# Biases carried inside the weights: a one in place of normalized xn's first feature

## The chip, the cores and the metric

The kernel runs on one core of a Trainium2 chip, in float32 for all products. The metric is the device time of one execution in microseconds. A core has these engines: TensorE (PE, matrix products; its weight loads are shown apart as PEld), VectorE (DVE, elementwise work and reductions), ScalarE (ACT, activation functions and copies with scale and bias), GpSimd (POOL, elementwise work) and SyncE (SP, which here only issues DMA transfers). Each takes its own instructions in order. SBUF is the on-chip memory. PSUM holds what TensorE produces[...].

## The reference

The source `x` has 4 batches of 2048 tokens with 256 features. Everything is computed from the row-normalized tokens `xn = layernorm(x)`. Two branches read them and their product is added to `x`:

```
x = src;  xn = layernorm(x)                    # per token, over 256 features, no scale and shift
q = xn @ Wq + bq;  k = xn @ Wk + bk;  v = xn @ Wv + bv     # 16 heads of 64
Q = elu(q) + 1;  K = elu(k) + 1
KV = sum over tokens of K v^T                  # per batch and head, 64 x 64
Z = 1 / (Q . (sum over tokens of K) + 1e-6)
o = Q KV Z;  attn = o @ Wo + bo
x1 = layernorm(xn + attn) * g1 + be1
s = layernorm(x1 + gelu(x1 @ W1 + b1) @ W2 + b2) * g2 + be2
g = silu(fp4_linear(silu(fp4_linear(xn, w_gate)) * fp4_linear(xn, w_up), w_down))
out = x + s * g
```

`fp4_linear` rounds both operands to a 4-bit grid with one scale for every 16 elements. This linear attention needs a whole batch's KV and key sums before any of that batch's queries can be finished.

Two facts of the reference matter. The mean of a row of `xn` over its features is zero, so its first feature is minus the sum of the others. And `elu(z) + 1` equals `max(z + 1, min(exp(z), 1))`.

## The kernel before, in words

**Tiling.** The 8192 tokens are cut into 32 blocks of 256 tokens (two tiles of 128, `TB` = 2), eight blocks per batch. Work on keys is done in two halves `f` of 512 of the 1024 key features. In PSUM, four buffers with the tag "mm" serve in turn nearly all products, and four hold sums over many products (`pxk` of a half, and the FFN's sums).

**Keys.** For a batch, the kernel does not form v. It sums `xn^T K` over all tokens (`pxk`, 256 by 512 per half) and multiplies by Wv afterwards. `key_product` makes pk = xn Wk for one tile and half (two matmuls of 512 columns), DVE adds bk + 1 (row `k<-pk,bk`, line 495) and ACT takes Exp of k − 1 (line 497). `key_elu` takes min with 1 and max with k on DVE (`kk`, line 504), and GpSimd adds kk to `kacc` (lines 506 and 508), an elementwise running sum that is later summed over its 128 partitions. `key_xk` multiplies xn^T by kk onto `pxk`.

**End of a batch's keys.** `m_of_half` (line 540) turns the sums of one half into `m`, which applied to Q gives attention already multiplied by Wo. ACT copies pxk to `xk`; TensorE sums kacc over partitions with a column of ones (`pks`, line 562); ACT copies the row to `krow`; SyncE stores it to `k_d` in DRAM and loads it back spread over all partitions (`ksum`). From ksum DVE builds `own`, `kcol` and the columns of `kh`, which give the denominators by matmul (`pz`). TensorE multiplies xk by Wv (`pkv`), eight small DVE operations add bv times ksum (`kv`, line 600), TensorE multiplies by Wo (`pm`), ACT copies to `m`. It is a generator: `step` moves it to its next `yield`, and so a few products at a time stand between the others.

**Queries.** `q_of` (line 763) makes four PSUM tiles pq for a block, each of two 128-feature columns. ACT copies each with its bias, bq + 1 (Identity, line 782, two per tile), into `q1`, takes Exp (line 785), and DVE takes min and max (`zq`, line 789). `q1` has three buffers, which keys and queries share.

**Stages.** A prologue works the keys of batch 0 in eight steps, with the quantizing of the gate and up weights between (to about 131 us). A transition makes the first `m` and starts block 0 (to about 185 us). Blocks 0 to 23 each carry two half-blocks of the keys of the next batch beside their own attention and FFN (some 57 us each). Blocks 24 to 31 have no keys beside them (some 44.5 us each).

**The xn of the next batch.** `keys_norm` normalizes a block of keys on DVE and stores it to DRAM as `xn_d`, from where the queries and the second half f load it again. `keys_xnT` (prologue) transposes it on TensorE. `keys_apart` and `keys_T` (later) do that by splitting float32 into 16-bit halves (`apart`, on ACT) and by transposing DMA transfers.

**Order.** TensorE takes instructions in program order. For DVE and ACT a scheduler keeps program order through the prologue, and from line 1040 (`in_order[0] = False`) chooses by priority; `tc.issue_after(i)` keeps an instruction behind another. Transfers stand in one SyncE queue. `load_when(dep, ...)` (line 129) holds a transfer back until `dep` is done: a one-element GpSimd copy writes into its destination first. Rows of the profile with L115 are DVE or ACT operations recorded by a helper, L99 matmuls, L102 transposes on TensorE.

Of the kernel before, what the change touches and what calls it, by code (L numbers as in the profile page):

```python
# [22 lines left out]
def linear_attention_gated_by_fp4_ffn(  # L23
# [23 lines left out]
):  # L47

# [93 lines left out]
    bk1 = const.tile([P, HD], F32, name="bk1")  # L142

    def load_wk(f, eng):
        fs = slice(f * HALF, (f + 1) * HALF)
        eng.dma_start(wk_sb[:, :, fs], wk_r[:, :, fs])
        eng.dma_start(bk1[:, fs], as_rows(bk[fs]))

    load_wk(0, nc.scalar)
    load_x(1)  # L150
    load_wk(1, nc.scalar)

# [10 lines left out]
    ones = const.tile([P, P], F32, name="ones")  # L163
# [29 lines left out]
    def w2_sums():  # L193
# [8 lines left out]
        2: [lambda dep: load_when(dep, wq_sb, by_chunks(Wq))],  # L202
        3: [lambda dep: load_when(dep, w1_sb, by_chunks(W1))],
        4: [
            lambda dep: load_row("g1", g1, dep),
# [4 lines left out]
        5: [lambda dep: load_w2(dep)],  # L210
    }

# [8 lines left out]
    def small_constants():  # L221


        vs = (("bq", bq), ("b1", b1), ("bv", bv), ("g1", g1), ("be1", be1))
        n = sum(v.shape[0] // P for _, v in vs)
        brow = work.tile([n, P], F32, tag="z", name="brow", bufs=1)
        r = 0
        for name, v in vs:
            k = v.shape[0] // P
            nc.sync.dma_start(brow[r : r + k, :], v.rearrange("(c p) -> c p", p=P))  # L230
            cols[name] = (r, r + k)
            r += k
        yield
        pb = mm_tile("pb")
        tr(pb[:, :n], brow, ident[:n, :n])
        bcol = const.tile([P, n], F32, name="bcol")
        vector.tensor_copy(bcol, pb[:, :n])
        for name, (lo, hi) in cols.items():
            cols[name] = bcol[:, lo:hi]
        vector.tensor_scalar(cols["bq"], cols["bq"], 1.0, None, ALU.add)  # L240
        yield
# [168 lines left out]

    def keys_norm(n, mv, rstd):

        xn = work.tile([P, TB, D], F32, tag="xn_k", name=f"xn_k_0_{n}", bufs=3)
        normalize(xn, x_k.pop(n), mv, rstd)
        xn_d[n] = dram.tile([P, TB, D], F32, tag="xn_d", name=f"xn_d_{n}")
        nc.sync.dma_start(xn_d[n], xn)
        return xn

    def keys_xnT(n, xn):
        xnT = work.tile([P, ND, T], F32, tag="xnT_k", name=f"xnT_k_0_{n}", bufs=3)  # L420
        scalar.copy(xnT, transposes(xn, f"k_{n}"))
        store_xnT(n, xnT)
        return xnT
# [18 lines left out]
    def keys_apart(b, sub, issue=None):  # L442

        f, bi = divmod(sub, NB)
        if f > 0:
            return
        n = b * NB + bi
        half = keys[b, sub][0].bitcast(U16).rearrange("p j (c f h) -> p h c j f", c=ND, h=2)
        apart = work.tile([P, 2, ND, TB, P], U16, tag="e", name=f"apart_{n}", bufs=3)
        with tc.issue_after(issue) if issue is not None else nullcontext():  # L450
            for h in range(2):
                scalar.copy(apart[:, h], half[:, h])
        apartT = work.tile([P, 2, ND * T], U16, tag="kk", name=f"apartT_{n}", bufs=3)
        nc.sync.dma_start(
            apartT.rearrange("p h (m t) -> p (h m) t", t=P),
            apart.rearrange("p h c j f -> p (h c j f)"),
            transpose=True,
        )
        keys[b, sub].append(apartT)

    def keys_T(b, sub, issue=None):

        f, bi = divmod(sub, NB)
        if f > 0:
            return
        n = b * NB + bi
        xn, *apartT = keys[b, sub]
        xnT = work.tile([P, ND, T], F32, tag="xnT_k", name=f"xnT_k_0_{n}", bufs=3)
        if apartT:
            with tc.issue_after(issue):  # L470
                scalar.copy(
                    xnT.bitcast(U16).rearrange("p c (t h) -> p h (c t)", h=2), apartT[0]
                )
        else:
            scalar.copy(xnT, transposes(xn, f"k_{n}"))
        store_xnT(n, xnT)
        keys[b, sub] = [xn, xnT]

    def key_sums(b, f, tag):
        keys[b, "acc", f] = batch.tile([P, HALF], F32, tag="kacc", name=f"kacc_{b}_{f}")  # L480
        keys[b, "pxk", f] = [acc_tile(f"pxk_{b}_{f}_{d}", tag) for d in range(ND)]

    def key_product(xnT, f, j, nm):

        fs = slice(f * HALF, (f + 1) * HALF)
        pk = mm_tile(f"pk_{nm}_{j}")
        for c in range(ND):
            mm(
                pk, xnT[:, c, j * P : (j + 1) * P], wk_sb[:, c, fs],
                start=c == 0, stop=c == ND - 1,  # L490
            )
        k1 = work.tile([P, HALF], F32, tag="q1", name=f"k1_{nm}_{j}", bufs=3)

        with tc.issue_after(keys["kh"]) if "kh" in keys else nullcontext():
            vector.tensor_tensor(k1, pk, bk1[:, fs], ALU.add)
        e = work.tile([P, HALF], F32, tag="e", name=f"ek_{nm}_{j}", bufs=3)
        keys["exp"] = scalar.activation(e, k1, AF.Exp, bias=neg_one).ins
        return k1, e

    def key_elu(b, f, k1, e, nm, first):  # L500

        kacc = keys[b, "acc", f]
        kk = work.tile([P, HALF], F32, tag="kk", name=f"kk_{nm}", bufs=3)
        ins = vector.scalar_tensor_tensor(kk, e, 1.0, k1, ALU.min, ALU.max)
        if first:
            acc = nc.gpsimd.tensor_copy(kacc, kk)
        else:
            acc = nc.gpsimd.tensor_tensor(kacc, kacc, kk, ALU.add)  # L508
        pool["last"] = acc.ins
        return kk, ins.ins  # L510
# [5 lines left out]
    def keys_k(b, sub):  # L516
# [5 lines left out]
        for j in range(TB):  # L522
            nm = f"{b}_{sub}"
            kk, ins = key_elu(
                b, f, *key_product(xnT, f, j, nm), f"{nm}_{j}", bi == 0 and j == 0
            )
# [13 lines left out]
    def m_of_half(b, f, dep=None, ahead=False):  # L540
# [3 lines left out]
        fs = slice(f * HALF, (f + 1) * HALF)  # L544
        wv = batch.tile([P, ND, HALF], F32, tag="wv", name=f"wv_{nm}", bufs=1)
        load_when(dep, wv, by_chunks(Wv)[:, :, fs])
# [8 lines left out]
        kacc = keys.pop((b, "acc", f))  # L555
        pxk = keys.pop((b, "pxk", f))
        xk = batch.tile([P, ND, HALF], F32, tag="xk", name=f"xk_{nm}", bufs=1)
        for d in range(ND):
            scalar.copy(xk[:, d, :], pxk[d])

        pks = mm_tile(f"pks_{nm}")
        mm(pks[:1, :], ones[:, 0:1], kacc, start=True, stop=True)
        krow = work.tile([P, HALF], F32, tag="x1T", name=f"krow_{nm}", bufs=1)[:1, :]
        scalar.copy(krow, pks[:1, :])
        k_d = dram.tile([1, HALF], F32, tag="k_d", name=f"k_d_{nm}", bufs=2)
        nc.sync.dma_start(k_d, krow)
        yield
        ksum = work.tile([P, 4, P], F32, tag="x1", name=f"ksum_{nm}")
        nc.sync.dma_start(
            ksum, k_d.rearrange("o (c f) -> o c f", c=4).to_broadcast([P, 4, P])  # L570
        )

        own = work.tile([P, 4, P], F32, tag="kk", name=f"own_{nm}", bufs=3)
        kcol = small.tile([P, 4], F32, tag="kcol", name=f"kcol_{nm}")
        vector.tensor_tensor(own, ksum, ident.unsqueeze(1).to_broadcast([P, 4, P]), ALU.mult)
        vector.tensor_reduce(kcol, own, AX.X, ALU.add)
        for i in range(2):
            hs = slice(i * DH, (i + 1) * DH)
            r0 = 2 * f + i
            ins = vector.tensor_copy(kh[b][hs, 4 * f : 4 * f + 4, r0], kcol[hs, :])  # L580
            if f > 0:
                keys["kh"] = ins.ins
# [13 lines left out]
        for ci in range(4):  # L596
            for h in range(2):
                hs = slice(h * DH, (h + 1) * DH)
                c = 4 * f + ci
                vector.scalar_tensor_tensor(  # L600
                    kv[hs, ci, hs], ksum[hs, ci, hs], cols["bv"][hs, c : c + 1],
                    pkv[hs, ci, :], ALU.mult, ALU.add,
                )
# [159 lines left out]
    def q_of(n, first=None):  # L763
# [5 lines left out]
        for cc in range(0, NH, 2):  # L769
            pq = mm_tile(f"pq_{n}_{cc}").rearrange("p (c t) -> p c t", c=2)  # L770
            q1 = work.tile([P, 2, T], F32, tag="q1", name=f"q1_{n}_{cc}", bufs=3)
# [8 lines left out]
            for ci in range(2):  # L780
                c = cc + ci
                scalar.activation(
                    q1[:, ci, :], pq[:, ci, :], AF.Identity, bias=cols["bq"][:, c : c + 1]
                )
            scalar.activation(e, q1, AF.Exp, bias=neg_one)
            if first is not None and cc == 0:
                behind = first()
            with tc.issue_after(behind.ins) if behind is not None else nullcontext():
                vector.scalar_tensor_tensor(zq[:, cc : cc + 2, :], e, 1.0, q1, ALU.min, ALU.max)
# [169 lines left out]
    xn = keys_norm(0, *keys_stats(0))  # L959
    for f in range(2):  # L960
        fs = slice(f * HALF, (f + 1) * HALF)
        nc.gpsimd.tensor_scalar(bk1[:, fs], bk1[:, fs], 1.0, None, ALU.add)
        key_sums(0, f, ("pxk", "acc")[f])
    xnT = keys_xnT(0, xn)
    ready = weight = iter(())
    for n in range(NB):
# [7 lines left out]
        def elu(i):  # L974
            f, j = tiles[i]
            kk[i], _ = key_elu(0, f, *k[i], f"0_{n}_{f}_{j}", n == 0 and j == 0)
# [61 lines left out]
    step(m_0, 2)  # L1038
# [26 lines left out]
    for n in range(NBLK):  # L1065
# [6 lines left out]
        if subs:  # L1072
# [3 lines left out]
            if n == 0:  # L1076
                for sub in subs:
                    keys_T(b + 1, sub)
                step(m_0)
# [75 lines left out]
        for sub in next_subs[:1]:  # L1155
# [6 lines left out]
        for sub in next_subs[1:]:  # L1162
# [66 lines left out]
```

## Time and profile before

| what | value |
|---|---|
| median of 3 runs | 1924.25 us (1922.2 to 1924.47) |
| the profiled execution, its own time | 1924.93 us |
| its span | 1923.1 us |
| PE busy | 1892.4 us, 98% |
| PE weight loads busy | 1379.4 us, 72% |
| DVE busy | 1495.0 us, 78% |
| ACT busy | 804.0 us, 42% |
| POOL busy | 552.9 us, 29% |
| ACT table loads | 122, 156.5 us |
| POOL kacc sums | 120 × 1488 ns = 178.5 us, and 8 copies, 4.9 us |
| DVE k<-pk,bk | 128 × 687 ns = 87.6 us |
| ACT q<-pq,bcol | 256 × 468 ns = 106.7 us |
| PE pks | 16 records, 8.2 us |
| mean granted TensorE clock | 0.996 |

The span runs from the first to the last recorded event; the execution's own time has 1.8 us around it. A row of the profile names the line, the engine, the operation, what is written and what is read, the shape, how many there are, their busy time and mean duration, and then how long the engine stood idle just before them and what ended that. A line of a timeline gives start, length (first start to last end for several alike), engine, operation, and idle time before it with its releaser. One float32 matmul is recorded as two. Recorded matmul durations overlap, so the time from start to start tells what one takes from TensorE.

### The profile page before, as it was taken

How to read it: one execution, taken by the hardware profiler on the slowest of the kernel's cores; microseconds unless marked ns; L12 is line 12 of the kernel's file. 1: busy time of each engine (PE TensorE's matmuls, PEld its weight loads, DVE VectorE, ACT ScalarE, POOL GpSimd, SP SyncE). 2: the span in 40 equal slices, each digit the busy share in tenths (PEclk: the TensorE clock that was granted, in tenths of full speed). 3: DMA queues.
4: the chain of work that ended last, by engine and by line, in shares of the span. 5: the costliest groups of instructions: out<-in, count | busy, mean ns of one | idle time of the engine just before them, and what ended most of it. 6: DMA issues, size and time to landing. Idle time of an engine off the chain costs nothing. (4 is left out here: it accounts for less than half of the span.)

```text
span 1923.1 us, 24467 instructions
## 1 busy us (share of the span) xinstructions
PE 1892.4 (98%) x8788; PEld 1379.4 (72%) x8788; DVE 1495.0 (78%) x2554; ACT 804.0 (42%) x1384; POOL 552.9 (29%) x461
## 2 busy tenths in 40 slices
PE   9998999999999999999999999999999999999997
PEld 4445677767777777777777777777777678888876
DVE  6878687777778887877777878777777778888875
ACT  2324554334444345542344543454433343444442
POOL 4432332232323233322332322332222322222221
PEclk9999999999999999999999999999999999999999
DMA  4435555454434455644344553464442344445441
GB/s 150 139 95 125 119 103 98 107 104 98 93 63 94 112 100 125 135 81 99 83 87 80 117 109 96 94 130 109 80 91 69 69 81 87 81 84 93 86 84 41
DMA packets 225121, 187.12 MB, mean 97 GB/s; under 512 B 103364, under 2 KB 185568, under 8 KB 225000
## 3 DMA queue, kind: packets, MB, share of 16 engines
q1 hardware_dynamic: 224168, 183.99, 45.3%
q8 instruction: 69, 1.13, 0.3%
q10 hardware_dynamic: 832, 1.57, 0.3%
q14 instruction: 52, 0.43, 0.1%
HBM read 131.41 MB, written 31.54 MB: 85 GB/s over the span
## 5 line engine op out<-in xcount | busy, mean ns | idle before, releaser
L508 POOL TENSOR_TENSOR kacc<-kacc,kk 128x512 f32<-128x512 f32 x120 | 178.5, 1488 | 597.1 <-DVE kk L115 595.0
L99 PE MATMUL pg<-wgu,qT 128*128 128x352 f32 x1024 | 311.8, 463 | 5.9 <-DVE qT L115 5.4
L99 PEld LDWEIGHTS pg<-wgu,qT 128*128 128x128 f32 x1024 | 194.5, 191 | 125.7 <-issue 13.2
L379 POOL TENSOR_TENSOR rstd<-rstd,neg_half 128x2 f32<-128x2 f32 x96 | 72.7, 758 | 687.4 <-DVE rstd L115 622.2
L99 PE MATMUL pxk<-kk,xn_k 128*128 128x512 f32 x512 | 235.8, 599 | 3.1 <-DVE kk L115 3.0
L99 PE MATMUL pk<-wk_sb,xnT_k 128*128 128x512 f32 x512 | 232.0, 596 | 1.0 <-ACT xnT_k L115 1.0
L99 PE MATMUL pa<-m,zq 128*128 128x256 f32 x1024 | 226.6, 379 | 1.8 <-DVE zq L115 1.8
L99 PE MATMUL pf<-x1T,w_sb 128*128 128x256 f32 x1024 | 226.7, 379 | 0.0
L99 PE MATMUL pq<-xnT,wq_sb 128*128 128x256 f32 x1024 | 226.3, 379 | 0.2 <-ACT hT L115 0.2
L99 PEld LDWEIGHTS pa<-m,zq 128*128 128x128 f32 x1024 | 193.9, 190 | 38.6 <-issue 11.8
L99 PEld LDWEIGHTS pq<-xnT,wq_sb 128*128 128x128 f32 x1024 | 194.3, 190 | 26.9 <-ACT hT L115 0.6
L99 PEld LDWEIGHTS pf<-x1T,w_sb 128*128 128x128 f32 x1024 | 192.0, 190 | 25.5 <-issue 0.4
L115 ACT ACT_TABLE_LOAD x122 | 156.5, 1283 | 65.0 <-DVE k L115 52.1
L99 PE MATMUL pd<-wd,qT 128*128 128x256 f32 x768 | 172.9, 380 | 1.8 <-DVE qT L115 1.4
L99 PEld LDWEIGHTS pk<-wk_sb,xnT_k 128*128 128x128 f32 x512 | 97.7, 191 | 103.6 <-issue 96.7
L99 PEld LDWEIGHTS pxk<-kk,xn_k 128*128 128x128 f32 x512 | 92.5, 190 | 109.0 <-issue 77.0
L99 PEld LDWEIGHTS pd<-wd,qT 128*128 128x128 f32 x768 | 145.3, 190 | 27.3 <-DVE qT L115 3.3
L115 DVE SCALAR_TENSOR_TENSOR zq<-e,q 128x512 f32<-128x512 f32 x128 | 90.8, 720 | 70.5 <-ACT e L115 70.4
L115 ACT ACTIVATE h<-pg 128x352 f32<-128x352 f32 x128 | 58.9, 460 | 206.0 <-PE pg L99 206.0
L115 ACT ACTIVATE ek<-k,neg_one 128x512 f32<-128x512 f32 x128 | 89.8, 719 | 115.7 <-DVE k L115 115.5
L115 ACT ACTIVATE x1T<-pt_x,bcol 128x256 f32<-128x256 f32 x64 | 32.7, 561 | 248.7 <-PE pt_x L102 248.7
L115 ACT ACTIVATE hT<-pf,bcol 128x256 f32<-128x256 f32 x256 | 105.5, 472 | 64.3 <-PE pf L99 64.0
(133 smaller groups left out, 2813.0 us busy)
## 6 DMA issues: line engine op xcount, KB each, us to landing
zb<-z_d SPq DMA_DIRECT2D x128, 256.0 KB, 6.0
qT<-scale_d SPq DMA_DIRECT2D x248, 128.0 KB, 5.6
x_k<-in_L_attn_src_dram SPq DMA_DIRECT2D x32, 256.0 KB, 4.1
x<-in_L_attn_src_dram SPq DMA_DIRECT2D x32, 256.0 KB, 2.8
xn_d<-xn_k SPq DMA_DIRECT2D x32, 256.0 KB, 3.6
xn<-xn_d SPq DMA_DIRECT2D x32, 256.0 KB, 2.6
xnT_d<-xnT_k SPq DMA_DIRECT2D x32, 256.0 KB, 2.0
xnT<-xnT_d SPq DMA_DIRECT2D x32, 256.0 KB, 2.8
```

What stands on the lines that cost most here:

```text
L99: return tc.keep_in_program_order(nc.tensor.matmul(*args, **kw))
L115: ins = op(*args, **kw)
L379: pool["last"] = nc.gpsimd.tensor_tensor(rstd[:, j0:j1], rstd[:, j0:j1], neg_half[:, j0:j1], ALU.pow).ins
L508: acc = nc.gpsimd.tensor_tensor(kacc, kacc, kk, ALU.add)
```

## The change

A one takes the place of the first feature of xn wherever xn meets a weight of keys, queries or values. The first feature is minus the sum of the others, so the product is kept when row 0 of the weight is subtracted from every row; row 0 itself is then free and takes the bias. The product xn W then carries its bias: bk + 1 and bq + 1 for keys and queries, bv for values. Since the first column of xn is one, the first row of `xn^T K` is the sum of the keys over tokens.

- `ones_in` writes the ones (128 × 2 elements): on DVE for the first block, on ACT elsewhere, after the store of the true xn to `xn_d` and before the transposes (and before `apart`, in `keys_apart`; for a second half f there is only the one).
- `bias_in_row0` changes the weights: Wk on DVE at the start, Wq and Wv on GpSimd during the prologue. It takes two `tensor_tensor` of 128 × 512 and one row operation for a half. Wv is stored to DRAM (`wv_d`) after this and loaded from there. Rows come by `load_row0`, in place of bk1 and of bq and bv in `small_constants`.
- The first block is normalized twice: once as `xn_first` with ones, once for `xn_d`.
- The DVE add of bk, the ACT copies with bq, the GpSimd sums kacc, pks, krow, ksum, own and kcol are gone. Exp and min/max read pk and pq in PSUM.
- The key sum, row 0 of xk, goes to `k_d` and from there by two transfers of 64 × 4 single elements into `kh`. Two ACT copies take the place of the eight DVE operations that made kv.
- pm of half 0 is put before block 0's queries (`step(m_0, 3)`), and the extra step within block 0 goes. The product over c is summed in the order 1, 0. In blocks whose next keys are a second half, `keys_apart` comes behind `x1_T` for both.

```diff
+    def ones_in(xn, eng=None):
+        if eng is None:
+            scalar.copy(xn[:, :, 0], ones)
+        else:
+            eng.memset(xn[:, :, 0], 1.0)
...
+    def bias_in_row0(name, w, f, eng):
+        fs = slice(f * HALF, (f + 1) * HALF)
+        for c in (1, 0):
+            eng.tensor_tensor(w[:, c, :], w[:, c, :], row0[name][:, 0, fs], ALU.subtract)
+        bias = row0[name][:1, 1, fs]
+        if name == "v":
+            eng.tensor_copy(w[:1, 0, :], bias)
+        else:
+            eng.tensor_scalar(w[:1, 0, :], bias, 1.0, None, ALU.add)
...
+    def wv_bias(f):
+        bias_in_row0("v", wv_sb[f], f, nc.gpsimd)
+        wv_d[f] = dram.tile([P, ND, HALF], F32, tag=f"wv_d{f}", name=f"wv_d{f}", bufs=1)
+        nc.sync.dma_start(wv_d[f], wv_sb[f])
...
     later = {
         0: [lambda dep: load_row("bo", bo, dep)],
-        2: [lambda dep: load_when(dep, wq_sb, by_chunks(Wq))],
-        3: [lambda dep: load_when(dep, w1_sb, by_chunks(W1))],
+        1: [lambda dep: load_row0("q", Wq, bq, dep)],
+        2: [
+            lambda dep: load_when(dep, wq_sb, by_chunks(Wq)),
+            lambda dep: load_row0("v", Wv, bv, dep),
+        ],
+        3: [
+            lambda dep: load_when(dep, w1_sb, by_chunks(W1)),
+            lambda dep: load_wv(1, dep),
+            lambda dep: wq_bias(0),
+        ],
         4: [
+            lambda dep: wq_bias(1),
+            lambda dep: wv_bias(1),
+            lambda dep: load_wv(0, dep),
...
-        5: [lambda dep: load_w2(dep)],
+        5: [lambda dep: wv_bias(0), lambda dep: load_w2(dep)],
...
     def keys_xnT(n, xn, apart=False):
+        if not apart:
+            ones_in(xn)
...
     def keys_apart(b, sub, issue=None):
         f, bi = divmod(sub, NB)
+        with tc.issue_after(issue) if issue is not None else nullcontext():
+            ones_in(keys[b, sub][0])
...
     def key_product(xnT, f, j, nm):
-        for c in range(ND):
+        for c in (1, 0):
...
-        with tc.issue_after(keys["kh"]) if "kh" in keys else nullcontext():
-            vector.tensor_tensor(k1, pk, bk1[:, fs], ALU.add)
-        keys["exp"] = scalar.activation(e, k1, AF.Exp, bias=neg_one).ins
-        return k1, e
+        keys["exp"] = scalar.activation(e, pk, AF.Exp, bias=neg_one).ins
+        return pk, e
...
-        if first:
-            acc = nc.gpsimd.tensor_copy(kacc, kk)
-        else:
-            acc = nc.gpsimd.tensor_tensor(kacc, kacc, kk, ALU.add)
-        pool["last"] = acc.ins
...
-        pks = mm_tile(f"pks_{nm}")
-        mm(pks[:1, :], ones[:, 0:1], kacc, start=True, stop=True)
-        krow = work.tile([P, HALF], F32, tag="x1T", name=f"krow_{nm}", bufs=1)[:1, :]
-        scalar.copy(krow, pks[:1, :])
-        nc.sync.dma_start(k_d, krow)
+        nc.sync.dma_start(k_d, xk[:1, 0, :])
         yield
-        ksum = work.tile([P, 4, P], F32, tag="x1", name=f"ksum_{nm}")
...
+        cols_ = k_d.rearrange("o (c i p) -> i p (o c)", c=4, i=2)
         for i in range(2):
             hs = slice(i * DH, (i + 1) * DH)
+            nc.sync.dma_start(kh[b][hs, 4 * f : 4 * f + 4, 2 * f + i], cols_[i])
...
-                vector.scalar_tensor_tensor(
-                    kv[hs, ci, hs], ksum[hs, ci, hs], cols["bv"][hs, c : c + 1],
-                    pkv[hs, ci, :], ALU.mult, ALU.add,
-                )
+        for h in range(2):
+            hs = slice(h * DH, (h + 1) * DH)
+            scalar.copy(kv[hs, :, hs], pkv[hs])
...
-            for ci in range(2):
-                c = cc + ci
-                scalar.activation(
-                    q1[:, ci, :], pq[:, ci, :], AF.Identity, bias=cols["bq"][:, c : c + 1]
-                )
-            scalar.activation(e, q1, AF.Exp, bias=neg_one)
+            scalar.activation(e, pq, AF.Exp, bias=neg_one)
...
-                vector.scalar_tensor_tensor(zq[:, cc : cc + 2, :], e, 1.0, q1, ALU.min, ALU.max)
+                vector.scalar_tensor_tensor(zq[:, cc : cc + 2, :], e, 1.0, pq, ALU.min, ALU.max)
...
-    xn = keys_norm(0, *keys_stats(0))
+    st = keys_stats(0)
+    xn = work.tile([P, TB, D], F32, tag="xn_k", name="xn_first", bufs=3)
+    normalize(xn, x_k[0], *st)
+    ones_in(xn, vector)
+    bias_in_row0("k", wk_sb[:, :, :HALF], 0, vector)
+    keys_norm(0, *st)
+    bias_in_row0("k", wk_sb[:, :, HALF:], 1, vector)
...
-    step(m_0, 2)
+    step(m_0, 3)
...
-                step(m_0)
...
+        early = [sub for sub in next_subs[:1] if sub < NB]
+        for sub in early:
             keys_apart(bn + 1, sub)
         x1_T(n)
...
-        for sub in next_subs[1:]:
+        for sub in next_subs[len(early) :]:
             keys_apart(bn + 1, sub, blk[n]["act"])
```

## The prediction

> **What bounds the kernel now.** I read the page's busy line, then the slices, then the waits of TensorE, then the timelines around each wait.
>
> The page:
>
> ```profile
> PE 1892.4 (98%) x8788; PEld 1379.4 (72%) x8788; DVE 1495.0 (78%) x2554; ACT 804.0 (42%) x1384; POOL 552.9 (29%) x461
> ```
>
> TensorE is busy nearly throughout; every other engine has a fifth or more of the span free. Slices of 60 us (busy time of PE, PEld, DVE, ACT, POOL, then clock, DMA share, GB/s) say where it is not:
>
> ```profile
> 0.00:60.00 60.00, 56.88 (x158) 28.14 (x159) 43.78 (x84) 16.70 (x26) 24.87 (x36) 0.97 0.48 155
> 120.00:180.00 60.00, 52.59 (x234) 30.80 (x233) 43.43 (x83) 26.20 (x45) 15.91 (x13) 0.94 0.50 104
> 600.00:660.00 60.00, 59.90 (x298) 43.31 (x297) 49.08 (x94) 29.90 (x50) 15.86 (x15) 1.00 0.54 122
> 1560.00:1620.00 60.00, 57.95 (x314) 44.56 (x311) 47.90 (x81) 24.33 (x44) 10.85 (x9) 1.00 0.38 75
> 1860.00:1923.00 63.00, 51.31 (x303) 44.27 (x301) 39.36 (x70) 21.14 (x39) 16.26 (x14) 0.95 0.22 53
> ```
>
> In the long middle (blocks 0 to 23, the 600 slice stands for it) TensorE has 0.1 us of 60 free: only fewer matmuls can shorten it. Free time lies at the start, in the change from prologue to blocks (120:180), at block 24 (1560) and at the end. TensorE's waits in 100:190, then in 1560:1923 (total, times, longest):
>
> ```profile
> PE pg L99 <- DVE qT L115: 5.4, 1, 5.4
> PE pxk L99 <- DVE kk L115: 3.0, 3, 1.5
> ...
> PE pz L99 <- DVE zq L115: 3.1, 5, 1.1
> PE pa L99 <- DVE zq L115: 1.8, 2, 1.6
> ```
>
> [...] a 256-column matmul is recorded with 379 ns, yet 32 of pa pass in 7.07 us, starts 0.22 us apart. I price matmuls by starts. [...] at 249.55 two hs sums took 3.44 us beside GpSimd's kacc sums, 0.68 us each without. [...]The k_d store issued at 145.28 released SyncE's next transfer at 147.04, 1.76 us later.
>
> **The change, part by part**, against the profiled execution's span of 1923.1 us (its own time is 1924.93, 0.7 above the median of 1924.25; I carry the difference to the median).
>
> *Matmuls removed.* The row sums pks go. The timeline of TensorE around one:
>
> ```profile
> 134.07 1.64 PE L99 MATMUL pg<-wgu,qT 128*128 128x352 f32 x5
> 135.64 1.02 PE L99 MATMUL pks<-kacc,ones 128*1 128x512 f32 x2
> 136.59 1.75 PE L99 MATMUL pg<-wgu,qT 128*128 128x352 f32 x5
> ```
>
> 136.59 − 135.64 = 0.95 us each (two records, fp32). Eight halves: 7.6 us, 1.9 of them in 120:180 and 5.7 in the full middle, where nothing can take their place but a wait. All other matmuls keep number and order; only pm of half 0 moves, ahead of pq of block 0.
>
> *Work removed elsewhere.* k adds 87.6 us (DVE), 256 q copies 106.7 (ACT), kacc 178.5 + 4.9 (POOL), own, kcol, kh 16.5 and kv 17.8 (DVE; 16 ACT copies replace the last). In the middle these lie beside a full TensorE: nothing directly. Without that cover DVE's share alone would be worth over 100 us, which is not on offer.
>
> *PSUM held longer.* Exp and min/max now read pk and pq themselves, so a "mm" buffer is freed at the min/max instead of the copy. With the min/max ends of this trace against the start of the matmul that reuses the buffer four tiles later, at least 1.0 us remains in the middle: 0. It is short in block 0 (3.1 to 4.1 us, inside the transition below) and block 31.
>
> *Start.* Before the first pk the weight's half 0 needs two 128x512 subtractions and one row on DVE, and the first normalize is done twice. The extra weight rows land no later than the bias rows did (7.3 us) and the second normalize is behind. The first pk, at 8.8 us, comes 0 to 2 us later; 2 × 0.69 by the row k<-pk plus a row is the whole price, most of it beside a TensorE that is still slow (0.85 us a matmul there against 0.43 later): **+0.4**.
>
> *Prologue, removed waits.* pxk waits 1.37 us at 113.4 and 1.49 at 122.1 for kk, behind k adds on a loaded DVE: **−2.9** (0 if another DVE operation is late instead).
>
> *Prologue, added waits.* A one is written over xn after its store has been read, by ACT, ahead of the transposes: normalize, store, landing (1.8 us by k_d; the page's median for xn_d is 3.6), one, transposes. Behind it on ACT stand the Exps of the next tiles. GpSimd also does six row operations on wq and the two halves of wv, each behind a load; the rstd of blocks 4 and 5 queue behind them, and with these DVE's normalize. SyncE gets two stores of wv. Prologue steps are about 16 us long (131 us for 8) and keys are prepared a block ahead, which covers most; **+1.5** (0 to 4).
>
> *Transition.* SyncE's timeline:
>
> ```profile
> 147.91 0.80 SPq L678 DMA_DIRECT2D qT<-scale_d  x2
> 154.27 0.40 SPq L134 DMA_DIRECT2D wo<-in_L_attn_Wo_dram  x1
> 154.71 2.87 SPq L678 DMA_DIRECT2D qT<-scale_d  x6
> 157.68 8.09 SPq L687 DMA_TRANSPOSE gridT<-grid  x1
> ```
>
> wo of half 1 waits until pm of half 0 is done (152.24 to 154.24); behind it wait six qT transfers and gridT, and TensorE stands from 163.38 to 168.74. After the change pm follows pkv at once. Count on: pkv ends 143.62 − 1.9 = 141.7; two kv copies on ACT, 0.47 each by the row q<-pq, with an xk copy (0.53) perhaps ahead: pm starts about 143.2, ends 145.2; scaleT 145.7, its store 146.1, landing 147.9, eight qT issues of 0.46 to 151.6, gridT 8.1 to 159.7, the multiply 160.4. Grid itself is ready earlier, since DVE loses own, kcol, kh and kv (5.7 us between 144.4 and 153.6). TensorE arrives at 163.38 − 1.9 + 1.5 = 163.0: no wait. So −5.4 − 1.9 + 1.5 = **−5.8** (−1.9 if something else keeps gridT, such as the two kh transfers of 4-byte elements on this queue[...]; no row here shows one. −7.3 if pm costs nothing). If gridT still comes last, its lateness beyond 163 counts.
>
> *Middle.* **−5.7**. The ones add waits on ACT. Its timeline in block 1:
>
> ```profile
> 259.93 1.14 ACT L115 COPY apart<-xn_k 128x512 uint16<-128x512 uint16 x2 [11.08 <-DVE mv L115]
> 262.41 1.02 ACT L115 ACTIVATE x1T<-pt_x,bcol 128x256 f32<-128x256 f32 x2 [1.34 <-PE pt_x L102]
> ```
>
> Now the order is one, apart, x1T, and the one waits for the xn_d store issued at 259.9: 259.9 + 1.8 = 261.7, the one at most 0.25 (a 128x128 copy takes that), apart 1.14, x1T 1.02: 264.1. TensorE wants x1T at 264.11. With a landing of 2.7 it would be 0.9 late, with 3.6 1.8 late. Against that, DVE comes earlier: 2.1 us less hs time without kacc, of which pa (ending at 253.9) passes on about 0.4. This happens in ten blocks (1, 2, 7 to 10, 15 to 18): I take 0.1 each, **+1** (0 to 18).
>
> *Blocks 24 to 30.* Without keys, pz follows pq closely; the q copies wait for q1's three buffers, freed by zq. In block 24 pz and pa wait 2.1 us, of which one copy's 0.94 (two of 0.47) goes and some of the rest: **−1.2** (0 to −2.1). In blocks 25 to 30 pz's 16 matmuls take 1.71 us where 1.07 is usual: 6 × 0.6 = **−3.5** (0 to −3.9).
>
> *Tail.*
>
> ```profile
> 1868.81 3.62 PE L99 MATMUL pf<-x1T,w_sb 128*128 128x256 f32 x16
> 1870.94 2.96 DVE L115 SCALAR_TENSOR_TENSOR zq<-e,q 128x512 f32<-128x512 f32 x3
> 1872.84 1.74 PE L99 MATMUL pz<-zq,kh 128*32 128x256 f32 x12 [0.41 <-DVE zq L115]
> ```
>
> DVE reaches zq of block 31 only at 1870.94, after o; until then pq's buffers stay held, and pf of block 30 (started 1868.81) wants one: pf and pz come about **+1.4** later (0 to 3).
>
> Sum: 0.4 − 2.9 + 1.5 − 5.8 − 5.7 + 1 − 1.2 − 3.5 + 1.4 = −14.8. Span 1923.1 − 14.8 = 1908.3; median 1924.25 − 14.8 = **1909.4**.
>
> **Rivals.**
> (1) Only the matmuls count. A later wait takes the place of gridT's (TensorE's arrival is but 2.6 us behind it), pz keeps waiting since DVE's zq still needs Exp first: 0.4 − 2.9 + 1.5 − 7.6 + 1 + 1.4 = −6.2, **1918**. For it: DVE is the releaser in every wait listed. Against: wo's hold on the queue is plainly ended by the move of pm.
> (2) No change. Removed work was hidden, and new waits eat the pks: prologue +4, tail +3, start +1, the middle's ones nearly hidden: **1924**. For it: TensorE never waits for most of what goes.
> (3) Slower. The one on ACT is late for x1T: each of ten blocks loses the store's landing beyond 1.8 us. With the page's 3.6 that is +18 in place of +1, and the prologue, which waits for the same stores, +4 in place of +1.5: 1909.4 + 17 + 2.5 = **1929**. It decides from a landing of about 3.2 us, lateness 1.4 per block. Against: xn_d's landing there is reckoned without other queues' loads, and DVE comes earlier.
> (4) More. Prologue additions cost nothing, pm's wait hides, the tail is free: −14.8 − 1.5 − 1.5 − 1.4 − 1 = −20, **1904** or a little below.
>
> **How the numbers follow.** The sum, 0.54, own range 1905 to 1914; rival 1, 0.20; rival 2, 0.08; rival 3, 0.10; rival 4, 0.08. Faster by over 0.2% (3.8 us, about what a measurement of this kernel tells from no change) are the sum, rivals 1 and 4: 0.82; same 0.08; slower 0.10. Leaving out rivals 2 and 3 and the far end of 4: 1902 to 1920.
>
> **What would show it.** pks gone and the 600 slice shorter by nothing else; pg after the transition not waiting for qT; SyncE issuing gridT about 6 us earlier; pxk without waits for kk at 113 and 122. Against the sum: TensorE's pf waiting for x1T, with ACT's idle before ones put on an xn_d store; pt_k waiting for DVE or POOL between 30 and 100 us; pz still 1.7 us long in blocks 25 to 30; pf of block 30 waiting by more than 3 us for a buffer.

## The result and the profile after

The changed kernel takes 1907.58 us (median of 4 runs, 1906.73 to 1908.44), the kernel before 1923.68 (4 runs): a ratio of 0.9917, 95% interval 0.9900 to 0.9934, 16.1 us less. The forecast was 1909.4. The profiled execution took 1906.97 us, its span is 1904.9, 18.2 us shorter than the one before. The profile before lies 1.2 us above its median and the one after 0.6 below, which makes most of the difference between 18.2 and 16.1.

The page's busy line, in the order of the one before:

```profile
PE 1875.4 (98%) x8772; PEld 1379.3 (72%) x8772; DVE 1303.2 (68%) x2338; ACT 708.9 (37%) x1191; POOL 357.5 (19%) x348
```

DVE lost 192 us, ACT 95 and POOL 195, TensorE 17. The span followed TensorE. The slices (same columns as before; the later ones are moved by 15 to 18 us, so that they hold about the same work):

```profile
0.00:60.00 60.00, 56.36 (x158) 28.40 (x159) 37.21 (x80) 16.57 (x30) 15.49 (x33) 0.97 0.53 173
120.00:180.00 60.00, 54.45 (x263) 34.53 (x262) 42.00 (x64) 24.84 (x45) 8.41 (x6) 1.00 0.46 98
180.00:240.00 60.00, 55.89 (x214) 37.75 (x213) 38.40 (x63) 24.32 (x41) 11.32 (x9) 0.97 0.48 96
600.00:660.00 60.00, 59.12 (x293) 43.54 (x293) 39.22 (x74) 25.83 (x43) 10.68 (x11) 1.00 0.55 118
1545.00:1605.00 60.00, 59.89 (x331) 47.26 (x330) 46.98 (x75) 21.65 (x37) 12.36 (x10) 1.00 0.42 87
```

Block 24 (1545) has lost its gap. The transition (120:180) is 5.6 us short of full where it was 7.4 short: its long wait has gone, but shorter ones have come. 180:240, which had 58.03 us busy before, has a new gap, and the 600 slice is 0.9 us short where it was 0.1. TensorE's waits in 100:190, then in 180:1540, then in 1540:1905 (pg is the product with the gate and up weights, pf and py are the two FFN products; pt_k, pwd and pscale are transposes, of the keys' xn, of w_down and of scales):

```profile
PE pm L103 <- issue: 1.9, 1, 1.9
PE pt_k L106 <- DVE zq L119: 1.2, 1, 1.2
PE pwd L106 <- DVE w_down L119: 0.9, 1, 0.9
...
PE pg L103 <- issue: 2.2, 1, 2.2
PE pq L103 <- ACT hT L119: 1.0, 1, 1.0
PE pf L103 <- ACT x1T L119: 0.9, 1, 0.9
...
PE pf L103 <- DVE zq L119: 2.7, 1, 2.7
```

The waits for qT (5.4), kk (3.0) and, in pz, for zq (3.1) are gone. TensorE runs its matmuls in nearly the same order in both kernels, so I took the start of each matmul in both traces and followed the difference. "issue" means that the profile shows no releaser; the timelines below show what TensorE waited for.

| stretch, times of before | forecast | measured |
|---|---|---|
| start and prologue, to 122 us | −1.0 | −4.1 |
| transition, to 185 | −5.8 | −4.5 |
| end of block 0, to 231 | 0 | +4.5 |
| middle, to 1536 | −4.7 | −7.2 |
| block 24, to 1564 | −1.2 | −3.5 |
| blocks 25 to 30, to 1835 | −3.5 | −3.6 |
| tail | +1.4 | +0.4 |
| sum | −14.8 | −18.0 |

The sum came near the forecast by terms that were off in both directions. The new loss is in the end of block 0. ScalarE's timeline there, then SyncE's, then TensorE's, all of the kernel after:

```profile
202.68 0.84 ACT L119 ACTIVATE hT<-pf,bcol 128x256 f32<-128x256 f32 x2
206.75 0.19 ACT L119 COPY xn_k<-ones 128x2 f32<-128x2 f32 x1 [3.23 <-DMA xn_d<-xn_k]
206.85 0.47 ACT L119 ACTIVATE hT<-pf,bcol 128x256 f32<-128x256 f32 x1
207.22 1.12 ACT L119 COPY apart<-xn_k 128x512 uint16<-128x512 uint16 x2
```
```profile
203.24 0.38 SPq L474 DMA_DIRECT2D xn_d<-xn_k  x1
203.73 0.37 SPq L708 DMA_DIRECT2D qT<-scale_d  x1
204.19 5.41 SPq L516 DMA_TRANSPOSE apartT<-apart  x2
209.65 3.41 SPq L708 DMA_DIRECT2D qT<-scale_d  x7
213.16 1.33 SPq L717 DMA_TRANSPOSE gridT<-grid  x1
```
```profile
217.36 3.70 PE L103 MATMUL pxk<-kk,xn_k 128*128 128x512 f32 x8
223.24 8.14 PE L103 MATMUL pg<-wgu,qT 128*128 128x352 f32 x21 [2.18 <-issue]
```

ACT stands 3.2 us for a store issued at 203.24, 3.5 us before. Behind it the split into `apart` is late; on SyncE the second apartT waits for that, and seven qT transfers and gridT wait behind apartT. DVE multiplies qT by gridT, and pg waits for the product. In the kernel before, ACT and SyncE had the same work here without a one:

```profile
211.63 1.14 ACT L115 COPY apart<-xn_k 128x512 uint16<-128x512 uint16 x2 [1.27 <-DVE xn_k L115]
212.85 1.23 SPq L454 DMA_TRANSPOSE apartT<-apart  x1
217.66 1.33 SPq L687 DMA_TRANSPOSE gridT<-grid  x1
```

`apart` starts 4.4 us earlier than there (207.22 for 211.63) and gridT is issued 4.5 us earlier, while TensorE is by now some 8 us ahead. Then the matmuls run at half speed for a while: windows of the same trace, clock in the third column from the end:

```profile
224.00:227.50 3.50, 3.50 (x8) 2.09 (x7) 2.97 (x4) 0.46 (x1) 0.00 (x0) 0.52 0.11 37
227.50:232.00 4.50, 4.50 (x16) 2.85 (x15) 2.05 (x4) 0.93 (x2) 0.00 (x0) 0.99 0.56 114
```

### The profile page after: what moved, and what is told of

Its sections match the earlier page's. It is cut to its first block, busy times and chain, and to the rows that moved or that the text cites. A ratio compares the mean times of both kernels' runs of the same rounds, so it can differ in the third digit from the quotient of the medians.

```text
span 1904.9 us, 23848 instructions
## 1 busy us (share of the span) xinstructions
PE 1875.4 (98%) x8772; PEld 1379.3 (72%) x8772; DVE 1303.2 (68%) x2338; ACT 708.9 (37%) x1191; POOL 357.5 (19%) x348
## 4 chain that ended last, share of the span: by engine, by line
PE 90%; DVE 4%; DMA 2%; issue 1%; POOL 1%; ACT 0%; SPq 0%; POOLq 0%; ACTq 0%; DVEq 0%
PE pg L103 15%; PE pk L103 11%; PE pa L103 11%; PE pxk L103 11%; PE pf L103 11%; PE pq L103 11%; PE pd L103 8%; PE py L103 8%; PE pz L103 2%; DMA zb<-z_d 1%; DVE x L119 1%; DVE scale L119 1%; PE pt_x L106 1%; POOL rstd L430 1%; PE pm L103 1%
## 5 line engine op out<-in xcount | busy, mean ns | idle before, releaser
L103 PE MATMUL pxk<-kk,xn_k 128*128 128x512 f32 x496 | 227.4, 597 | 0.0
L119 DVE SCALAR_TENSOR_TENSOR kk<-ek,pk 128x512 f32<-128x512 f32 x128 | 85.9, 686 | 146.8 <-ACT ek L119 146.8
L119 DVE TENSOR_TENSOR h<-h,pg 128x352 f32<-128x352 f32 x128 | 66.1, 517 | 100.7 <-PE pg L103 99.2
L119 ACT ACTIVATE ek<-pk,neg_one 128x512 f32<-128x512 f32 x128 | 85.5, 686 | 110.0 <-PE pk L103 109.7
L103 PE MATMUL py<-w_sb,hs 128*128 128x128 f32 x1024 | 125.9, 275 | 0.0
```

The costliest lines, as they stand in the source:

```text
L103: return tc.keep_in_program_order(nc.tensor.matmul(*args, **kw))
L119: ins = op(*args, **kw)
```

## The experiments

All times are medians of runs; ratios are to the kernel before, with 95% intervals.

| kernel | median, us | ratio | interval |
|---|---|---|---|
| before, without pks | 1920.98 | 0.9985 | 0.9978 to 0.9991 |
| before, pm ahead | 1927.85 | 1.0022 | 1.0015 to 1.0029 |
| before, queries read in PSUM | 1925.03 | 1.0004 | 0.9996 to 1.0013 |
| before, keys read in PSUM | 1920.42 | 0.9978 | 0.9969 to 0.9986 |
| before, without kacc's sums | 1928.67 | 1.0024 | 1.0015 to 1.0034 |
| before, kv by ACT | 1921.15 | 0.9986 | 0.9979 to 0.9992 |
| before, kv by ACT, without pks | 1914.21 | 0.9947 | 0.9933 to 0.9960 |
| before, kv by ACT, pm ahead | 1921.92 | 0.9994 | 0.9986 to 1.0003 |
| changed, pm late | 1912.62 | 0.9941 | 0.9928 to 0.9953 |
| changed, no ones in block 0 | 1904.03 | 0.9895 | 0.9882 to 0.9909 |
| changed, two more normalizations | 1904.87 | 0.9898 | 0.9884 to 0.9911 |
| changed, one more, and queries of block 31 copied | 1904.47 | 0.9904 | 0.9890 to 0.9918 |

The first six are parts of the change made alone; what each leaves out is said with it. Against the medians of before that they were run beside (1923.69, 1923.94, 1923.21) they are worth −2.7, +4.2, +1.3, −3.3, +4.7 and −2.1 us: +2.1 together, where the whole change is worth −16.1.

### Without pks

```diff
-        pks = mm_tile(f"pks_{nm}")
-        mm(pks[:1, :], ones[:, 0:1], kacc, start=True, stop=True)
-        scalar.copy(krow, pks[:1, :])
+        scalar.copy(krow, xk[:1, 0, :])
```

> The kernel before without the eight pks sums; krow copies row 0 of xk instead, so the key sums are left out of the denominators; GpSimd still makes kacc. Theory (TensorE has no free time in the middle, so a removed matmul counts in full, and with it what stood around it): 1.15 to 1.5 us for each of six halves and 1.9 in the transition, where SyncE's hold moves with TensorE: -9 us. Rival (a wait takes their place, they were cheap as recorded): -4 us or less.

Measured −2.7, as the rival had it. The matmuls go (1.0 to 1.15 us each by the starts), but more than half is returned. In the transition pscale waits 1.7 us longer for its scales on DVE. In the middle the next half's end takes it back, once a batch. DVE and TensorE of this kernel:

```profile
628.94 0.69 DVE L115 SCALAR_TENSOR_TENSOR kk<-ek,k 128x512 f32<-128x512 f32 x1 [0.79 <-ACT ek L115]
629.55 2.33 DVE L115 SCALAR_TENSOR_TENSOR kv<-ksum,bcol,pkv 64x64 f32<-64x64 f32 x8
631.92 0.90 DVE L115 TENSOR_TENSOR qT<-qT,gridT 128x512 f32<-128x512 f32 x1
```
```profile
632.87 3.52 PE L99 MATMUL pg<-wgu,qT 128*128 128x352 f32 x11 [0.80 <-DVE qT L115]
```

pg starts when DVE's multiplication ends, and that stands behind eight kv operations. The prediction's "nothing can take their place but a wait" holds to the letter: a wait took their place.

### kv by ScalarE, alone and without pks

```diff
-        nc.sync.dma_start(ksum, k_d.rearrange(...).to_broadcast([P, 4, P]))
...
-        vector.tensor_tensor(own, ksum, ident.unsqueeze(1).to_broadcast([P, 4, P]), ALU.mult)
-        vector.tensor_reduce(kcol, own, AX.X, ALU.add)
...
-            ins = vector.tensor_copy(kh[b][hs, 4 * f : 4 * f + 4, r0], kcol[hs, :])
+            nc.sync.dma_start(kh[b][hs, 4 * f : 4 * f + 4, 2 * f + i], cols_[i])
...
-                vector.scalar_tensor_tensor(kv[hs, ci, hs], ksum[hs, ci, hs], ...)
+            scalar.copy(kv[hs, :, hs], pkv[hs])
```

> The kernel before with kh filled from k_d by two transfers and kv made by two ACT copies, so ksum, own, kcol and eight DVE operations go for each half; bv times the key sums is left out; pks stays. Theory (kv on DVE stands ahead of the multiplication with gridT and holds pg by 0.3 us once a batch; SyncE's hold behind wo stays): -1 to -2 us, the stall of 5.4 us for gridT still there. Rival (DVE's chain makes gridT late): the stall goes, -5 us or more.

> As the last, and without pks too (krow copies row 0 of xk, so the key sums are left out). Theory (alone, pks's gain was half returned in the middle, as pg then waits for the multiplication behind kv on DVE; with kv on ACT it is kept): 1.15 us for each half in the middle with nothing given back, -8 to -10 us against before, more than the two parts' own gains together. Rival (the parts only add): -3 to -5 us.

Measured −2.1 and −9.0, as the theory had both. The stall for gridT stayed at 5.4 us in both ("PE pg L99 <- DVE qT L115: 5.4, 1, 5.4"), so DVE's chain did not set it. From the first to the second, TensorE's starts move by 1.15 us at each of the six halves in the middle and nothing comes back. So pks is worth 2.7 us with kv on DVE and 6.9 with kv on ACT (1921.15 − 1914.21): each edit uncovers what the other hid. It is 1.15 rather than 0.95 because the first two py behind pks came 0.2 us later with it. The transition's 1.7 us for pscale is lost in the second kernel as well. (The second's interval runs from −7.7 to −12.9 us; the two parts alone, −4.8 together, lie outside it.)

### pm ahead of the queries: alone, with kv on ScalarE, and undone

```diff
-    step(m_0, 2)
+    step(m_0, 3)
...
-                step(m_0)
```

> The kernel before with pm of half 0 put ahead of block 0's queries, nothing else. Theory (the stall of 5.4 us for gridT and six slow matmuls behind it, 1.8 us, come from the order on the queue, but DVE makes kv only at 149.2 us, so pm now waits some 4 to 5.5 us in its new place): -1 to -3 us. Rival A (the order alone gives the transition's gain): -5.8 us. Rival B (gridT is late for DVE's work, not for the queue): 0, or slower by pm's wait.

> The kernel before with kv on ACT and kh by transfers, as in the first of these, and pm of half 0 ahead of block 0's queries; bv times the key sums is left out. Theory (the move pays only if kv is ready): pm waits 2 us in place of 3.9, the stall for gridT and the slow matmuls behind it go: -4 to -6 us against before. Rival (what pg then waited for, h on DVE, is as late): slower than before by 2 us or more, as with the move alone.

> The changed kernel with pm of half 0 back behind block 0's queries. Theory (SyncE is held by wo until pm is done, so gridT comes late again): TensorE waits again for qT in the transition, 4 to 7 us with slow matmuls behind it, and the wait of pm for kv, 2 us, goes: +3 to +5 us against the changed kernel. Rival (DVE's relief took the stall away, not the order): 0 to -2 us.

Measured +4.2, −1.3 and, against the changed kernel, +5.0. The first two missed what was expected; the third is at the edge of it. TensorE's longest waits in the first (125:240), then in the second:

```profile
PE pm L99 <- DVE kv L115: 3.9, 1, 3.9
PE pg L99 <- DVE h L115: 3.0, 1, 3.0
```
```profile
PE pg L99 <- DVE h L115: 2.4, 1, 2.4
PE pm L99 <- ACT kv L115: 2.3, 1, 2.3
```

In both the stall for gridT is gone, as expected: the order on the queue makes it. But alone the move costs more than it wins: pm waits for kv on DVE, and later pg waits 3.0 us for DVE's h, which multiplies by an earlier pg, a wait I had not expected, with slow matmuls behind each (eight pm in 3.12 us, 1.99 in before; ten pg in 4.92, sixteen in 5.00 from 136.59 on in before). With kv on ACT, pm's wait shrinks to 2.3, and the later one stays at 2.4, so the move gains nothing there (−1.3 with it, −2.1 without). The changed kernel has no such wait for h. Its DVE is free of the k adds (0.69 us each) and of kacc's slowing (hs sums of 0.68 us, 1.45 in before) too, which is the likely reason; no run adds these alone to the second kernel. The undone move shows the other side:

```profile
151.87 0.40 SPq L138 DMA_DIRECT2D wo<-in_L_attn_Wo_dram  x1
152.31 2.40 SPq L708 DMA_DIRECT2D qT<-scale_d  x5
154.81 6.37 SPq L717 DMA_TRANSPOSE gridT<-grid  x1
```

SyncE of the changed kernel with pm late: held by wo until 151.87, gridT at 154.81, and pg waits 4.9 us and runs slow after (eleven in 6.36 us, 32 in 9.96 in the changed kernel). In the changed kernel gridT issues at 149.19. So the move is worth 5 us within the whole change, nothing with kv alone off DVE, and is a loss by itself.

### Keys read in PSUM, and no kacc sums

```diff
-            vector.tensor_tensor(k1, pk, bk1[:, fs], ALU.add)
-        keys["exp"] = scalar.activation(e, k1, AF.Exp, bias=neg_one).ins
-        return k1, e
+        keys["exp"] = scalar.activation(e, pk, AF.Exp, bias=neg_one).ins
+        return pk, e
```
```diff
-            acc = nc.gpsimd.tensor_tensor(kacc, kacc, kk, ALU.add)
```

> The kernel before with Exp and min/max of the keys reading pk in PSUM; the 128 adds of bk on DVE are left out, and so is bk; GpSimd still sums kacc. Theory (k adds load DVE in the prologue, where pxk waits for kk): prologue shorter by 3 to 4 us, block 0 by up to 1, middle 0: -3.5 us. Rival (DVE was slowed there by GpSimd's kacc sums, not by the adds): within 1 us of before.

> The kernel before with the 120 GpSimd sums onto kacc left out (the 8 first copies stay), so the key sums are wrong by what is left out; k adds and pks stay. Theory (k adds on DVE set the prologue's waits): -1 us at most, hs sums near 0.7 us each in place of 1.45. Rival (kacc's sums slow DVE and so set the waits of pxk at 113 and 122 us): -3 to -4 us, all before 130 us.

Measured −3.3 and +4.7. Followed by the starts, the first wins 4.5 us by 122 us, much as expected, and gives half a microsecond back by the end. The second also wins in the prologue, 2.8 us between the first pk and 122 us (pxk's two waits), which only the rival expected. (From the first pk on its starts lie 1.5 us ahead of those of the kernel before, whose first four pk matmuls took 3.60 us, with a clock of 0.53 in 8.80:12.00; so do those of most of the other profiles. I leave this out of each gain by the starts.) Each edit alone ends the same waits, so their gains don't add: those waits needed both loads on DVE, the adds and the slowing by kacc (rstd at 108.47 of the kernel before took 1.18 us beside one of its sums, 0.17 at 116.82 without). hs sums fell to 0.68 us in the changed kernel from 1.45.

Then the second loses some 0.3 us a block in the middle, 6 us in all, which neither theory nor rival had. GpSimd and DVE of the kernel without kacc's sums:

```profile
273.53 1.60 POOL L758 TENSOR_TENSOR x<-x,shift_r 128x512 f32<-128x512 f32 x1
275.09 1.72 POOL L623 TENSOR_TENSOR xn<-xn,bo_r 128x512 f32<-128x512 f32 x1
```
```profile
276.00 1.36 DVE L115 SCALAR_TENSOR_TENSOR zq<-e,q 128x512 f32<-128x512 f32 x1 [0.32 <-ACT e L115]
277.28 0.68 DVE L115 TENSOR_TENSOR k<-pk,bk 128x512 f32<-128x512 f32 x1
```

Without kacc between them, GpSimd's sums for the next block move from 285 to 291 us forward to 272 to 277, where DVE's zq works: one zq takes 1.36 us instead of 0.69, the k add behind it is late, and kk, for which pxk waits. In the changed kernel GpSimd's sums sit there too (271.90 to 275.74), but no k add stands before kk, and zq, which reads one operand in PSUM there, takes 0.69 us beside them; pxk does not wait. No run tests whether the operand's place is what shortens zq.

### Queries read in PSUM

```diff
-            for ci in range(2):
-                scalar.activation(q1[:, ci, :], pq[:, ci, :], AF.Identity, bias=...)
-            scalar.activation(e, q1, AF.Exp, bias=neg_one)
+            scalar.activation(e, pq, AF.Exp, bias=neg_one)
...
-                vector.scalar_tensor_tensor(zq[...], e, 1.0, q1, ALU.min, ALU.max)
+                vector.scalar_tensor_tensor(zq[...], e, 1.0, pq, ALU.min, ALU.max)
```

> The kernel before with Exp and min/max of the queries reading pq in PSUM; the 256 copies with bq are left out, and so is bq. Theory (the copies, waiting for q1's three buffers, set pz's waits in blocks 24 to 30; elsewhere they are hidden): blocks 24 to 30 shorter by 6 to 7 us, pf of block 30 waits 2 to 3 us for a PSUM buffer and the end loses at most 0.5 of it: -6 us, and nothing between 240 and 1540 us. Rival (zq still needs Exp; nothing was won by the copies, and 3.1 us of pz came from elsewhere): within 1 us of before.

Measured +1.3, with 1 inside the interval: no gain, where −6 was expected. The stretch from block 24 to 30 wins 7.0 us by the starts, as the theory has it, and as the changed kernel does (7.1), so the rival's reason is wrong although its number is near. The gain is lost at both ends, which the theory had at 0.5 us at most. TensorE's waits in 125:240 and in 1540:1924:

```profile
PE pt_k L102 <- DVE zq L115: 3.0, 1, 3.0
...
PE pf L99 <- DVE zq L115: 2.7, 1, 2.7
```

Both are waits for a PSUM buffer that zq still holds. In the transition it is 3.0 us here, where DVE still makes own, kcol and kv ahead of zq, and 1.2 in the changed kernel; with slow matmuls behind it (eight pt_k in 1.71 us and eight pm in 3.09, 1.04 and 1.99 in before), it costs some 5 us here. In the tail both kernels wait 2.7 us at the same place, and yet the end loses 2.1 us here and 0.4 in the changed kernel, because the clock was 0.52 after the one wait and 1.00 after the other. The same wait can cost 1.7 us more; the last section has both. The remaining 1.7 us are 0.1 in most key blocks, at pxk.

### The ones that wait in block 0

```diff
+        if (b, sub) not in ((1, 2), (1, 3)):
             with tc.issue_after(issue) if issue is not None else nullcontext():
                 ones_in(keys[b, sub][0])
```

> The changed kernel without the ones that ACT writes in block 0 for the two key blocks of block 1, so bias and sums of these are wrong. Theory (ACT waits there 3.2 us for the store of xn_d, so that a transfer of apartT on SyncE and gridT behind it come late): pg of block 2 no longer waits (2.2 us), the slow matmuls behind that go (1.75 us), and pq waits less for hT (1.0): -4 us against the changed kernel. Rival (gridT is late for qT's transfers or the grid itself): within 1 us of the changed kernel.

```diff
         normalize(xn, x_k[n], mv, rstd)
+        kept = xn
+        if n in (NB + 2, NB + 3):
+            kept = work.tile([P, TB, D], F32, tag="xn_s", name=f"xn_s_{n}", bufs=2)
+            normalize(kept, x_k[n], mv, rstd)
...
-        nc.sync.dma_start(xn_d[n], xn)
+        nc.sync.dma_start(xn_d[n], kept)
```

> The changed kernel in which these two key blocks are normalized a second time into a tile of their own, from which xn_d is stored, so the ones wait for no store. Theory: -3 to -4 us against the changed kernel, 1.5 us more of DVE's work being hidden. Rival (DVE is what sets apartT's time there): 0 to +1.5 us.

Measured 3.6 and 2.7 us less than the changed kernel's median. TensorE at the place in question, without those ones:

```profile
217.14 3.70 PE L103 MATMUL pxk<-kk,xn_k 128*128 128x512 f32 x8
220.68 5.49 PE L103 MATMUL pg<-wgu,qT 128*128 128x352 f32 x18
```

pg follows pxk without a wait and at full speed; gridT issues at 210.07 in place of 213.16. So the wait of a copy of 128 × 2 elements cost about 4 us of the change's gain (by the starts 4.1). With a second normalization most of that stays won: pg waits 0.4 us here and pq 1.4 for hT (0.5 without the ones), but in the transition pg now waits 1.2 us for qT, which the changed kernel does not. This kernel leaves nothing of the reference out; its four runs (1903.54 to 1905.17) lie below all four of the changed kernel, though the two intervals against before overlap, and the two were not run side by side.

### One normalization more, and the tail

```diff
+        if n == NB + 3:
...
+            if n == NBLK - 1:
+                q1 = work.tile([P, 2, T], F32, tag="q1", name=f"q1_{n}_{cc}", bufs=2)
+                scalar.copy(q1, pq)
+                pq = q1
             scalar.activation(e, pq, AF.Exp, bias=neg_one)
```

> The changed kernel with a second normalization for one key block (the later of block 0's two), and with the queries of block 31 copied from PSUM by ACT first, so that PSUM is free for pf of block 30. Theory: -3.5 us for the first against the changed kernel (only the later block's apart set gridT), and in the tail pf's wait of 2.7 us goes, of which the end sees 0.5 us: 1903.5 us. Rival (the earlier block counts too, or the copies delay zq by as much): 1905 to 1907 us.

Measured 1904.47, no different from the last (one of the four runs took 1908.43). The first part works: block 0's end wins 3.7 us by the starts. In the tail the rival was right:

```profile
1846.67 3.62 PE L103 MATMUL pf<-x1T,w_sb 128*128 128x256 f32 x16
1851.28 0.64 PE L103 MATMUL pz<-zq,kh 128*32 128x256 f32 x8 [0.99 <-ACT q L119]
1852.76 0.62 PE L103 MATMUL pz<-zq,kh 128*32 128x256 f32 x4 [0.84 <-DVE zq L119]
1853.99 0.62 PE L103 MATMUL pz<-zq,kh 128*32 128x256 f32 x4 [0.60 <-DVE zq L119]
```

pf no longer waits, and comes 2.8 us earlier; pz, the next to need zq, waits for it in pieces and gives all of it back. zq's time on DVE sets the tail; the buffer only decided where TensorE waits.

## Why the prediction was right

The forecast's value, range and direction held (−14.8 against −16.1), and so did the mechanisms of its larger terms. That the value came so close is partly luck: a loss of 4.5 us in block 0 that no step had, and a transition 1.3 us short of its forecast, offset gains in the prologue, the middle and block 24 that were 7.9 us larger than reckoned. By its own steps:

- *Matmuls removed*, −7.6: the mechanism right, the size low. A half takes 1.15 us with the delay behind it, some 9 us in all. What the step missed is that pks counts in full only because kv leaves DVE in the same change; alone it was worth 2.7.
- *Work removed elsewhere*, "in the middle ... nothing directly": wrong for kv. pg behind it starts 0.37 us earlier once a half, and without the edit more than half of pks's gain is lost. The cover that I named, a full TensorE, was nearly used up at that one place.
- *PSUM held longer*, 0: right in the middle; the shortage in block 0, which the step had found, became a wait of 1.2 us for pt_k.
- *Start*, +0.4: the first pk comes 0.2 us later.
- *Prologue, removed waits*, −2.9: right place, measured −4.5 by the run that reads keys in PSUM, with a delay of 0.5 us at 104 us and some of 0.1 before it that I had not counted. The waits did not hang on the k adds alone: leaving out kacc's sums ended them too.
- *Prologue, added waits*, +1.5: next to nothing; the prologue as a whole is 4.1 shorter, against 4.5 for the keys in PSUM alone. GpSimd's twelve operations on the rows of Wq and Wv (17 us), the stores and the ones stayed covered. That the keys prepared a block ahead cover them is the prediction's reason; no run tests it.
- *Transition*, −5.8: the stall went as reckoned, and pm's wait was 1.9 where 1.5 was taken. Missing were the slow clock after the old stall (0.52 in 169:173 of the kernel before; −1.8), and on the other side pt_k (+1.2) and waits for the w_down transposes (+1.7). The two pwd waits appear alike in the kernel with kv on ACT and pm ahead, which has none of the new weights, and go when pm is put back in the changed kernel. So they don't come with the new weights. The move alone, which loses 4.2 us, does not show them either: they seem to need a TensorE that is early.
- *Middle, the ones*, +1 (0 to 18): 0.9, in one block, with a landing of 3.7 us, from a store issued at 601.11 to the one at 604.78. In the other nine no wait for x1T shows: the page's median from issue to landing of xn_d, 3.6 us before and the base of rival 3's price, is 2.0 after. The same wait for a landing struck harder where I hadn't looked: in block 0, outside the ten blocks, through SyncE's queue rather than through x1T, for +4.5. The step counted the ones' wait against x1T only, and not against the transfers behind `apart`.
- *Block 24*, −1.2: measured −3.5, and −2.8 in the run that changes the queries alone: all of pz's waits went, not one copy's part. kv on ACT alone wins 1.3 at the same place, so the two share this gain. *Blocks 25 to 30*, −3.5: −3.6. pz won 0.65 us in each, 3.9; a wait of pscale that came (1.4 us) about cancels pd's waits for qT that went (1.4).
- *Tail*, +1.4: pf waited 2.7 us, but pz then came without a wait, and no slow clock followed (1.00 in 1853:1856); +0.4. In the run with the queries alone one did (0.52 in 1870:1873), and the end lost 2.1.

Rival 1 (only the matmuls count) fell with the transition and blocks 24 to 30; rival 2 with all of them. Rival 3's mechanism came at two places, one of them outside its ten blocks, and at neither with its price of 1.8 us: 0.9 and 4.5.

## What to carry to other kernels

Removed work off the critical path pays where its removal lets another edit's gain through (pks was worth 2.7 us with kv on DVE, 6.9 with kv on ACT): price edits together, by asking for each gain what is late next, and whether the same change moves that too. When a small operation is put behind a store's landing (ACT stood 3.2 us for one here, and the end of block 0 lost 4.5), follow not only the next operation on that engine but each transfer that waits for what stands behind it, and all that is queued behind that transfer. A PSUM buffer held longer moves a wait rather than making one, as in the tail here (2.7 us of pf in the one kernel, 2.4 of pz in the other), if the same late operation feeds TensorE a moment later anyway.

## What the hardware showed unexpectedly

After some waits of TensorE, matmuls ran at half the rate: clock 0.52 in 224.0:227.5 of the changed kernel (wait 2.2 us), records of pg 0.59 us apart in place of 0.30 in the kernel before (wait 5.4). This added 1.7 to 1.8 us to the wait. It did not come each time. Here is pf of block 30 behind a wait of 2.7 us at the same place of the tail, in the kernel that reads queries in PSUM and then in the changed kernel, each with two windows around its start:

```profile
1869.74 5.41 PE L99 MATMUL pf<-x1T,w_sb 128*128 128x256 f32 x16 [2.68 <-DVE zq L115]
1865.00:1870.00 5.00, 2.32 (x11) 1.74 (x10) 4.41 (x7) 0.90 (x2) 4.61 (x4) 1.00 0.90 150
1870.00:1873.00 3.00, 3.00 (x9) 2.35 (x9) 1.48 (x3) 1.75 (x2) 0.23 (x1) 0.52 0.60 117
```
```profile
1853.06 3.72 PE L103 MATMUL pf<-x1T,w_sb 128*128 128x256 f32 x16 [2.67 <-DVE zq L119]
1848.00:1853.00 5.00, 2.39 (x12) 1.75 (x10) 4.41 (x8) 0.69 (x1) 4.29 (x4) 1.00 0.89 143
1853.00:1856.00 3.00, 2.94 (x14) 2.60 (x15) 1.80 (x4) 2.81 (x4) 0.54 (x1) 1.00 0.93 145
```

pf's sixteen matmuls took 5.41 us at a clock of 0.52 in the one and 3.72 at 1.00 in the other. In the window before, PE was busy for 2.32 and 2.39 of 5 us; these windows do not show why the two went apart. So a wait cost its length here, and in some places 1.7 to 1.8 us more. Since the same wait did both, a difference of 1.7 us between two profiles need not come from their edit.
